# Where the second layer's later work stands in TensorE's order: fixed slots, or slots chosen by running estimates

## The chip, the cores and the metric

One core of a Trainium2 chip runs the whole computation in one launch. The metric is the device time of one execution in microseconds, from start to end, as the median of several runs. Five engines work side by side and meet through semaphores: TensorE (PE in the profile: matrix products and transposes), VectorE (DVE: elementwise work, reductions, reading results out of PSUM), ScalarE (ACT: functions such as Exp, and copies), GpSimd (POOL) and SyncE (SP, which issues the DMA transfers). Each engine takes the instructions of its own queue in order.

## The reference

The input x has 16 batches of 64 rows and 512 columns; a context has 16 batches of 1601 rows. Six residual stages follow one another:

```python
x = x + _L0_xattn_ref(_layernorm(x), ctx_1024, ...)
x = x + _L0_attn_ref(_layernorm(x), ...)
x = x + _L0_ffn_ref(_layernorm(x), ...)
x = x + _L1_xattn_ref(_layernorm(x), ctx_1024, ctx_1024, mask, ...)
x = x + _L1_attn_ref(_layernorm(x), ...)
x = x + _L1_ffn_ref(_layernorm(x), ...)
```

The first three (layer 0) are not touched here. The fourth is a cross attention with 16 heads of 32 columns over the 1601 context rows of the batch, with a mask, biases on all projections, and softmax. The fifth is a "differential" attention: each row forms a 32 by 32 table of products between its own 32 query groups and 32 key groups of 16 numbers, takes softmax along it, subtracts a learned multiple of one half from the other, multiplies with v, normalises, and goes through Wo; a LayerNorm and a feed-forward network (512 to 2048 to 512, with Relu) follow inside the same stage. The sixth is a feed-forward network with ternary weights (every weight rounded to -1, 0 or 1 times a scale), activations rounded to 8 bits with a scale for each row, and a convolution over three neighbouring rows and Silu between its two products:

```python
h = bit_linear(x, w1)
h = depthwise_conv1d(h.transpose(0, 2, 1), conv_w, conv_b).transpose(0, 2, 1)
return bit_linear(silu(h), w2)
```

## The kernel before

The layer-0 functions run first. Then `l1_layer` does the last three stages. Two batches make one tile t of 128 rows, so 16 batches b make 8 tiles. PE's instructions keep the order in which the program names them (`tc.manual_schedule(engines={PE})`). The queues of the other engines are put in order by a scheduler when the kernel is built, by its own estimate of when each instruction could start; after that every queue is fixed.

**The cross attention** is a run of 32 calls of `step(b, F, ...)`, two for each batch. F picks half of the heads: four score tiles p of 128 rows (two heads of 64 queries) by 1601 keys. A step does the following on PE, in this order:

- `turn` (transposes by `transpose_keys`, L182, copied out by ACT, L185) and `last_keys` (L888) turn the first two p tiles of the step before; blocks of `project_v` (products `wkv,ctxT` at L146, evacuated at L832) stand between; `attend` (L898) multiplies the weights with V into a bank of tag acc.
- `scores` runs four times, once for each piece of the keys (three of 384 and one of 449). It takes two PSUM banks of tag tp and two of tag mm and writes products of queries and keys into them (L873); DVE copies them into p where the mask allows it (`copy_predicated`, L880), which frees the banks. Tag tp has two banks, mm four, acc two. The transposes take tp banks too. V blocks and the turning of the other two p tiles stand between the four.
- a second `attend`, and when F is 0 the end of the batch before, `finish`: a small product that spreads the softmax sums (`fold`, L924), a multiplication on DVE that divides by them (oT, L934), on odd batches (so in the step of an even b) a bias on DVE (L940), then the output product py (L146 with `w,oT`), and `residual`.
- `weigh` for each p tile: the negative maximum of the rows on DVE (negm, L1318), then Exp on ACT (L1319). And 16 pieces of `project_k` (L803, evacuated by ACT at L811): keys for the next step.

**The later stages** of a finished tile are a generator, `later(t)`: LayerNorm, the q, k, v products (L146 with `w,hT`), 16 pairs of DVE instructions for q times k (`products`: a multiplication at L967 and a reduction at L968), the softmax along 32 (L1010 to L1033, with Exp on ACT at L1019), 8 pairs for att times v, the normalisation (ending at L1063), Wo, a LayerNorm, the feed-forward network with W1 and W2 (L1100), and the mark "fed". Then `last(t)`: LayerNorm and rounding, four parts of the ternary product (hs at L1207, a product with the middle tap on ACT into y at L1213, the two other taps on DVE at L1220 and L1224, Silu at L1230, a maximum at L1232), the largest value of each row over all parts (top, L1238, transposed at L1244), rounding (L1255, L1256) and the second ternary product (L1266) and the output. `queries(t)` makes the queries of the next tile, and `ternary_weights` rounds the ternary weights once, during the first batches.

Each `yield` ends a piece of such a generator. A `slot()` inside `step` runs one piece of `behind`, whatever the engines are doing; in the F=0 step of an even batch there are no slots before the batch's `finish` has run (`resting`), where `behind` is set to the `later` of the tile just finished. Where a piece depends on a slow step, additional bare `yield`s leave slots empty. At the end of each odd batch whatever is left of `behind` is run at once. In the last two batches one slot in three is left empty and `behind` stops at the mark "attended". The loops at the end of `l1_layer` take turns between the last tile (`final`, t=7) and the rest of the one before it.

The lines that the steps below speak of most:

```python
def slot():
    nonlocal places
    places += 1
    if resting == 0 and (b < B - 2 or places % 3):
        run(behind, 1)
```

Of the kernel before, what the change touches and what calls it, by code (L numbers as in the profile page):

```python
# [19 lines left out]
P = 128  # L20
# [13 lines left out]
EPS = 1e-5  # L34
# [403 lines left out]
def until(steps, mark):  # L438

    for x in steps:  # L440
        if x == mark:
            return
        yield
# [244 lines left out]
def l1_layer(g, d, out):  # L688
# [5 lines left out]
    with ExitStack() as es:  # L694
# [76 lines left out]

        def value_tile():
            nonlocal taken
            i = taken % (NV + 5)
            taken += 1
            if i < NV:
                return vpool.tile([P, 2, 256], F32, tag="v", name="v")
            return g.const.tile([P, 2, 256], F32, tag=f"x{i - NV}", name="v")
# [18 lines left out]
        def project_k(b, h):  # L797

            for n, (_, w) in enumerate(KC):
                for f in (h, h + 2):  # L800
                    ps = mm(g)
                    for c in range(NC):
# [4 lines left out]
                        if c == 1:  # L807
                            yield
                    tag = "kT" if n < 3 else "kT_last"
# [5 lines left out]
        def project_v(b, half):  # L815

            for k in range(0, len(KT), 2):
# [3 lines left out]
                for j, (k0, kw) in enumerate(blocks):  # L821
# [6 lines left out]
                    vs[b, half, k + j] = v[:kw, j, :]  # L828
                    if j + 1 < len(blocks):
                        yield  # L830
# [3 lines left out]

        def queries(t):

            u = apool.tile([P, D], F32, tag="u2", name="u")
            ln_apply(g, u, g.x[t], ln_stats(g, small, [g.x[t]]), 0)
            yield
            yield  # L840
            uT = apool.tile([P, NC, P], F32, tag="u2T", name="uT")
            nc.scalar.copy(uT, transpose4(g, u))
            yield
# [20 lines left out]
        def scores(b, F, n, ps_, mk):  # L864
# [5 lines left out]
            for r in range(4):  # L870
                for i in range(2):
# [6 lines left out]
                    )  # L878
            for p, bank in zip(ps_, banks):
                nc.vector.copy_predicated(p[:, k0 : k0 + w], mk[:, k0 : k0 + w], bank[:, :w])  # L880

        def last_keys(ps_, pTs):
# [4 lines left out]
            for j, p in enumerate(ps_):  # L887
                nc.tensor.transpose(pt[:kw, j, :], p[:, k0 : k0 + kw], g.ident)  # L888
                pTs[j].append(pT[:kw, j, :])
# [4 lines left out]


# [65 lines left out]
        def products(q, k, out, n):  # L961

            kv = k.rearrange("p (j d) -> p j d", d=16).unsqueeze(1).to_broadcast([P, CH, 32, 16])
            for i in range(n // CH):
# [5 lines left out]
                )  # L970
                yield

        def norm_T(src, gname, bname):

            z = apool.tile([P, D], F32, tag="z", name="z")
            ln_apply(g, z, src, ln_stats(g, small, [src]), 0)
            for _ in range(4):
                yield
            pt = transpose4(g, z)
            dst = apool.tile([P, NC, P], F32, tag="hT", name="hT", bufs=2)  # L980
# [7 lines left out]
        def later(t):  # L988

            u = apool.tile([P, D], F32, tag="u", name="u")  # L990
            ln_apply(g, u, g.x[t], ln_stats(g, small, [g.x[t]]), 0)
            yield
            hT = yield from norm_T(u, "ln1_g", "ln1_b")
            yield
            qkv = []
            for n, s in (("q", float(DA) ** -0.5), ("k", 1.0), ("v", 1.0)):
# [5 lines left out]
                yield  # L1002
# [9 lines left out]
            nc.vector.copy_predicated(raw, nan, zero.to_broadcast([P, 32 * 32]))  # L1012
            yield
# [4 lines left out]
            )  # L1018
            nc.scalar.activation(att, att, AF.Exp)  # L1019
            yield  # L1020
            yield
# [9 lines left out]
            yield  # L1031
            a2 = att[:, :HA, :HA]
            nc.vector.tensor_tensor(a2, a2, att[:, HA:, HA:], ALU.subtract)  # L1033
            yield
# [12 lines left out]
            nc.vector.tensor_tensor(o3, o3, inv.unsqueeze(2).to_broadcast([P, HA, 32]), ALU.mult)  # L1047
            sq = apool.tile([P, D], F32, tag="z", name="sq")
            nc.scalar.activation(sq, o, AF.Square)
            yield  # L1050
# [4 lines left out]
            nc.vector.tensor_scalar(r, r, 1e-6, None, ALU.max)  # L1055
            nc.scalar.activation(r, r, AF.Sqrt)
            yield
# [6 lines left out]
            for _ in range(4):  # L1064
                yield
            oT = apool.tile([P, NC, P], F32, tag="hT", name="oT", bufs=2)
            nc.scalar.copy(oT, transpose4(g, o))
            yield
# [4 lines left out]
            yield  # L1073
# [7 lines left out]
            for k in range(5):  # L1081
                if k < 4:
# [8 lines left out]
                    for f in range(4):  # L1091
                        nc.scalar.activation(
                            hids[k][:, f, :], ps[:, f, :], AF.Relu, bias=col(g, "b1", 4 * k + f)
                        )
                    yield
                if k > 0:
                    for f in range(4):
# [5 lines left out]
                        )  # L1103
                    yield
            nc.vector.tensor_tensor(g.x[t], po, g.x[t], ALU.add)
            yield "fed"
# [4 lines left out]
        def ternary_weights():  # L1111


            for n, name in enumerate(("w1T", "w2T")):
# [5 lines left out]
                for k in range(8):  # L1120
                    nc.vector.tensor_reduce(
                        part[:, k : k + 1], load(k), AX.XY, ALU.add, apply_absolute_value=True
                    )
                    yield
# [7 lines left out]
                for k in range(8):  # L1132
# [4 lines left out]
                    nc.vector.tensor_scalar(wb, w, MAGIC, None, ALU.subtract)  # L1137
                    dst = g.tern[4 * n + k // 2].rearrange("p (c n) -> p c n", c=NC)
# [38 lines left out]
        def last(t):  # L1177
            u = apool.tile([P, D], F32, tag="z", name="u")
            ln_apply(g, u, g.x[t], ln_stats(g, small, [g.x[t]]), 0)
# [10 lines left out]
            yield  # L1190
            yield
# [6 lines left out]
            yield  # L1198
            big = apool.tile([P, 4, P], F32, tag="u", name="big")
            sT = []  # L1200
            for k in range(4):
                w = load_ternary(k)
                ps = mm(g).rearrange("p (f x) -> p f x", f=4)
                for f in range(4):
# [364 lines left out]
```

## Time and profile before

| | us |
|---|---|
| three timed runs | 3416.5, 3417.17, 3418.84 |
| median | 3417.17 |
| the profiled execution | 3425.22 |
| its span in the trace | 3423.4 |
| layer 0, about | 0 to 830 |
| layer 1, about | 830 to 3423 |
| mean granted clock of PE | 0.961 |

The profiled execution is 8.05 us longer than the median. In the profile, a busy row gives an engine's time at work and its share of the span. Rows of a timeline give start, duration, engine, line, operation, written tile `<-` read tiles, shape and count (merged when equal instructions follow one another; the duration then is from the first start to the last end); in brackets is the idle time before the row and what ended it. Waits list an engine's line, what it waited for, total time, how often, and the longest. `PEclk`, or the granted clock, is the share of full clock speed that TensorE had.

### The profile page before, as it was taken

How to read it: one execution, taken by the hardware profiler on the slowest of the kernel's cores; microseconds unless marked ns; L12 is line 12 of the kernel's file. 1: busy time of each engine (PE TensorE's matmuls, PEld its weight loads, DVE VectorE, ACT ScalarE, POOL GpSimd, SP SyncE). 2: the span in 40 equal slices, each digit the busy share in tenths (PEclk: the TensorE clock that was granted, in tenths of full speed). 3: DMA queues.
4: the chain of work that ended last, by engine and by line, in shares of the span. 5: the costliest groups of instructions: out<-in, count | busy, mean ns of one | idle time of the engine just before them, and what ended most of it. 6: DMA issues, size and time to landing. Idle time of an engine off the chain costs nothing.

```text
span 3423.4 us, 51470 instructions
## 1 busy us (share of the span) xinstructions
PE 3125.6 (91%) x22000; PEld 2099.7 (61%) x22008; DVE 1624.4 (47%) x2614; ACT 1083.6 (32%) x1960; POOL 380.6 (11%) x339
## 2 busy tenths in 40 slices
PE   6999999898999999989998999999899999999816
PEld 3344445586677667667766766666677667667604
DVE  2121214113733754392467348454825773484285
ACT  1111011111333344333433343343334343433303
POOL 0000002243011010010101001100110010001000
PEclk9999999999899999999999999999999999999958
DMA  9988502596531214213320522242133205120405
GB/s 358 318 285 301 195 25 93 208 336 196 184 84 45 91 38 152 74 48 111 109 68 24 157 69 85 62 128 81 42 118 102 78 27 158 59 79 13 144 16 173
DMA packets 272293, 422.34 MB, mean 123 GB/s; under 512 B 22576, under 2 KB 168112, under 8 KB 272064
## 3 DMA queue, kind: packets, MB, share of 16 engines
q1 hardware_dynamic: 258928, 372.38, 33.4%
q0 software_dynamic: 13136, 46.67, 3.9%
q8 instruction: 173, 2.83, 0.3%
q14 instruction: 56, 0.46, 0.0%
HBM read 394.36 MB, written 24.64 MB: 122 GB/s over the span
## 4 chain that ended last, share of the span: by engine, by line
PE 64%; DVE 24%; DMA 4%; ACT 3%; issue 3%; POOL 1%; SPq 1%; POOLq 0%; ACTq 0%; DVEq 0%
PE ps_mm L146 26%; PE ps_mm L803 12%; DVE prod L967 7%; PE ps_acc L146 7%; DVE att L968 5%; PE ps_acc L1100 3%; PE ps_tp L182 3%; DVE negm L1318 3%; PE ps_mm L240 3%; DVE p L880 2%; PE ps_tp L873 2%; DVE o L968 2%; PE ps_acc L274 2%; PE ps_acc L898 2%; DMA ck<-in_ctx_dram 2%
## 5 line engine op out<-in xcount | busy, mean ns | idle before, releaser
L146 PE MATMUL ps_mm<-wkv,ctxT 128*128 128x256 f32 x2304 | 544.5, 384 | 1.0 <-DVE p L880 1.0
L803 PE MATMUL ps_mm<-ctxT,wkv 128*128 128x384 f32 x1536 | 520.2, 489 | 0.0
L146 PEld LDWEIGHTS ps_mm<-wkv,ctxT 128*128 128x128 f32 x2304 | 422.5, 191 | 91.6 <-issue 41.0
L803 PEld LDWEIGHTS ps_mm<-ctxT,wkv 128*128 128x128 f32 x1536 | 285.9, 191 | 181.7 <-issue 8.5
L1301 POOL MEMSET p<- 128x1601 f32 x128 | 184.1, 1441 | 1777.9 <-PE ps_tp L182 1105.8
L880 DVE COPY_PREDICATED p<-mk,ps_tp 128x384 f32<-128x384 uint8 (+1 forms) x256 | 143.9, 599 | 449.0 <-PE ps_mm L873 448.1
L832 ACT COPY v<-ps_mm 128x512 f32<-128x512 f32 (+1 forms) x224 | 123.0, 551 | 464.1 <-PE ps_mm L146 463.6
L185 ACT COPY pT<-ps_tp 128x512 f32<-128x512 f32 x384 | 206.7, 589 | 157.2 <-PE ps_tp L182 157.2
L146 PE MATMUL ps_mm<-wkv,ctxT_last 128*128 128x256 f32 (+1 forms) x1024 | 248.3, 386 | 1.0 <-ACT v L832 1.0
L182 PE MATMUL ps_tp<-ident,p 128*128 128x128 f32 x1640 | 217.8, 275 | 14.1 <-DVE p L880 9.1
L1318 DVE TENSOR_REDUCE negm<-p 128x1 f32<-128x1601 f32 x128 | 226.5, 1810 | 1.1
L1319 ACT ACTIVATE p<-p,negm 128x1601 f32<-128x1601 f32 x128 | 208.4, 1628 | 51.5 <-DVE negm L1318 49.5
L182 PEld LDWEIGHTS ps_tp<-ident,p 128*128 128x128 f32 x1640 | 191.2, 142 | 54.1 <-issue 18.5
L146 PEld LDWEIGHTS ps_mm<-wkv,ctxT_last 128*128 128x128 f32 (+1 forms) x1024 | 172.4, 178 | 72.2 <-issue 40.4
L803 PE MATMUL ps_mm<-ctxT_last,wkv 128*128 128x449 f32 x512 | 201.7, 539 | 0.0
L967 DVE TENSOR_TENSOR prod<-qkv 128x1024 f32<-128x1024 f32 x128 | 156.6, 1223 | 91.0 <-ACT qkv L1000 87.4
L811 ACT ACTIVATE kT<-ps_mm,cols 128x384 f32<-128x384 f32 x192 | 108.8, 574 | 192.5 <-PE ps_mm L803 192.5
L968 DVE TENSOR_REDUCE att<-prod 128x64 f32<-128x1024 f32 x128 | 155.9, 1218 | 3.9
L803 PEld LDWEIGHTS ps_mm<-ctxT_last,wkv 128*128 128x128 f32 x512 | 96.1, 190 | 87.1 <-issue 79.5
L898 PE MATMUL ps_acc<-pT,v 128*32 128x64 f32 (+1 forms) x6656 | 116.2, 228 | 32.0 <-ACT pT L185 31.0
L880 DVE COPY_PREDICATED p<-mk,ps_mm 128x384 f32<-128x384 uint8 (+1 forms) x256 | 138.8, 591 | 0.0
L898 PEld LDWEIGHTS ps_acc<-pT,v 128*32 128x32 f32 (+1 forms) x6656 | 103.5, 115 | 56.6 <-ACT pT L185 33.0
(302 smaller groups left out, 4003.3 us busy)
## 6 DMA issues: line engine op xcount, KB each, us to landing
ctxT<-in_ctx_T_dram SPq DMA_DIRECT2D x48, 1024.0 KB
ck<-in_ctx_dram SPq DMA_DIRECT2D x48, 1024.0 KB
ctxT<-in_ctx_T_dram SPq DMA_DIRECT2D x48, 768.0 KB
w<-in_W1T_dram SPq DMA_DIRECT2D x64, 512.0 KB
w<-in_W2T_dram SPq DMA_DIRECT2D x64, 512.0 KB
wt<-tern SPq DMA_DIRECT2D x64, 512.0 KB
ctxT_last<-in_ctx_T_dram SPq DMA_DIRECT2D x16, 898.0 KB
w<-in_x_Wq_dram SPq DMA_DIRECT2D x16, 512.0 KB
```

The source lines that it names most:

```text
L146: g.nc.tensor.matmul(out, lhsT=lhs(c), rhs=rhs(c), start=(c == 0), stop=(c == n - 1))
L182: g.nc.tensor.transpose(pt[:kw, j, :], p[:, k0 + j * P : k0 + j * P + kw], g.ident)
L185: (out_of or (lambda o, i: evac(g, o, i)))(pT[:kw, :blocks, :], pt[:kw, :blocks, :])
L803: nc.tensor.matmul(ps[:, :w], lhsT=wk[:, c, ts(f, P)], rhs=ctxs[b, n][:, c, :], start=(c == 0), stop=(c == NC - 1),)
L832: nc.scalar.copy(v[:kw, : len(blocks)], ps[:kw, : len(blocks)])
L880: nc.vector.copy_predicated(p[:, k0 : k0 + w], mk[:, k0 : k0 + w], bank[:, :w])
L898: nc.tensor.matmul(po[ts(r, HDX), ts(f, S)], lhsT=vs[b, f // 2, k][:, ts(4 * (r % 2) + 2 * (f % 2) + r // 2, HDX)], rhs=pTs[r // 2][k][:, ...
L967: nc.vector.tensor_tensor(pr, qv.unsqueeze(2).to_broadcast([P, CH, 32, 16]), kv, ALU.mult)
L968: nc.vector.tensor_reduce(out[:, ts(i, CH * 32)], pr.rearrange("p i j d -> p (i j) d"), AX.X, ALU.add)
L1301: nc.gpsimd.memset(p, -1e15)
L1318: nc.vector.tensor_reduce(negm, p, AX.X, ALU.max, negate=True)
L1319: nc.scalar.activation(p, p, AF.Exp, bias=negm, accum_out=sums[b][:, at : at + 1])
```

## The change

The fixed placing of the pieces is replaced by a running estimate. `g.now` is an estimate of PE's time and `g.dve` one of the time up to which DVE is loaded. Parts of the program add their own constants: `pe(us)` moves `g.now`; `dv(us)` moves `g.dve` from the later of both. A piece now ends with nothing, with a time before which the next may not be placed (`done()` after DVE's load, `soon()` after PE's time), or with a mark. A class `Work` holds a generator with its time; `may(backlog)` says whether its next piece may be placed: its time has come, and DVE's load is no more than `backlog` ahead of PE. A slot runs up to two pieces, of `asked` (the queries), else `old` (the end of the tile before), else `behind`.

Beside this:

- `norm` replaces the LayerNorm helpers in these stages and cuts them at ACT's Sqrt; pieces end ahead of ACT's steps in softmax and normalisation.
- The four ternary parts are put a step apart: seven steps, each with Silu of part step-2, the product of part step, the convolution of part step-1 and the maximum of part step-3. y alternates between the tags prod and att; the fourth sT goes to tag hT.
- `later(t-1)` is no longer run to its end at the end of an odd batch. At `finish` it is run on up to the mark "topped", then goes on as `old` while the next tile's `later` starts as `behind`; `old` is run to its end at the same place in the next batch.
- `weigh` of the four tiles moves from ahead of and between the first K pieces to the K pieces 2, 4, 6 and 8; the second part of `finish` moves to K piece 2; more slots stand between V blocks, each with its own backlog.
- `fetch` of a later tile's rows moves from the start of an even batch to the F=0 step of an odd one.
- The loops at the end are one loop: a piece of `final` has the first call until its mark "fed", then waits until the rest of the tile before is over.

The diff, cut to its core:

```diff
+class Work:
+    def __init__(self, g, steps):
+        self.g, self.steps, self.at, self.mark, self.over = g, iter(steps), 0.0, None, False
+        self.passed = set()
+    def may(self, backlog):
+        g = self.g
+        return not self.over and g.now >= self.at and g.dve - g.now <= backlog
+    def step(self):
+        x = next(self.steps, self)
+        self.over = x is self
+        self.passed.add(x if isinstance(x, str) else None)
+        self.mark = x if isinstance(x, str) else None
+        self.at = x if isinstance(x, float) else 0.0
+        if self.mark:
+            self.at = max(self.g.dve + 0.4, self.g.now + 1.6)
+    def rest(self, mark="over"):
+        while not self.over and mark not in self.passed:
+            self.g.now = max(self.g.now, self.at)
+            self.step()
...
+        def pe(us):
+            g.now += us
+        def dv(us):
+            g.dve = max(g.dve, g.now) + us
+        def done(us=0.1):
+            return max(g.dve, g.now) + us
+        def soon(us):
+            return g.now + us
...
@@ products
                 )
+                dv(2.5)
                 yield
...
@@ later: softmax
+            dv(2.5)
+            yield done()
             nc.scalar.activation(att, att, AF.Exp)
-            yield
-            yield
+            yield soon(2.2)
...
@@ last
-            for k in range(4):
-                w = load_ternary(k)
...
+            for step in range(7):
+                k = step - 2
+                if 0 <= k < 4:
...
+                    nc.scalar.activation(sT[k], y[k].rearrange("p f b s -> p f (b s)"), AF.Silu)
+                k = step
+                if k < 4:
+                    w = load_ternary(k)
...
+                k = step - 1
+                if 0 <= k < 4:
...
+                k = step - 3
+                if k >= 0:
+                    nc.vector.tensor_reduce(
+                        big[:, k, :], sT[k].rearrange("p f t -> p t f"), AX.X, ALU.max,
+                        apply_absolute_value=True,
                     )
+                    dv(0.8)
+                yield done(0.2 if 0 < step < 5 else 1.2)
             top = spool.tile([P, P], F32, tag="dg", name="top")
             nc.vector.tensor_reduce(top, big.rearrange("p f t -> p t f"), AX.X, ALU.max)
-            yield
-            yield
-            yield
-            yield
+            dv(0.8)
+            yield "topped"
...
@@ step
+            def slot(backlog=2.6):
+                nonlocal named
+                for _ in range(2):
+                    if asked.mark != "ready" and asked.may(backlog):
+                        asked.step()
+                    elif old.may(backlog):
+                        old.step()
+                    elif (
+                        not (behind.mark == "normed" and not old.over)
+                        and not (b >= B - 2 and behind.mark == "attended")
+                        and (b < B - 2 or g.now >= named + 2.5)
+                        and behind.may(backlog)
+                    ):
+                        named = g.now
+                        behind.step()
...
             for i in range(3):
                 value()
-                slot()
+                slot(1.6)
+                value()
+                slot(1.0)
                 if i == 2 and before is not None:
                     last_keys(p4[2:], tail)
-                value()
+                    value()
                 if before is not None:
                     turn(p4[2:], pTs, i)
-                value()
+                    slot(0.6)
+                if i < 2 or before is None:
+                    value()
                 scores(b, F, i + 1, ps_, mk)
+                slot(2.6)
...
-            weigh(0)
             slot()
-            run(keys, 2)
-            weigh(1)
-            if F == 0:
-                run(ending)
...
+            for i in range(16):
+                if i == 2 and F == 0:
+                    run(ending)
+                    pe(3.5)
+                    pos[b] = mm(g, tag="acc")
+                    if b % 2 == 0 and b > 0:
+                        behind.rest("topped")
+                        old, behind = behind, Work(g, later(b // 2 - 1))
+                    if b % 2 == 1:
+                        old.rest()
+                    if b % 2 == 1 and b + 1 < B:
+                        if 2 <= b // 2:
+                            fetch(b // 2 + 1)
+                        asked = Work(g, queries(b // 2 + 1))
+                if i >= 2 and F == 1 and asked.mark == "ready":
+                    asked.step()
+                    asked.step()
                 run(keys, 1)
+                if i in (2, 4, 6, 8):
+                    weigh(i // 2 - 1)
+                slot(3.2)
...
-            final = later(NT - 1)
-            feed = until(rest, "fed")
-            for _ in until(final, "attended"):
-                run(feed, 1)
-            run(feed)
-            for _ in until(final, "fed"):
-                run(rest, 3)
-            while next(final, final) is not final:
-                run(rest, 2)
-            run(rest)
+            final = Work(g, later(NT - 1))
+            passed, fed = set(), False
+            while not (final.over and behind.over):
+                if final.may(1.2) and (behind.over or "fed" not in passed):
+                    final.step()
+                    passed.add(final.mark)
+                elif behind.may(1.2) and ("attended" in passed or not fed):
+                    behind.step()
+                    fed = fed or behind.mark == "fed"
+                else:
+                    g.now += 0.1
```

## The prediction

> **What bounds the kernel now.** I read the page's busy shares first, then a table of stretches, then PE's waits, then the timelines around the longest of them. The shares:
>
> ```profile
> PE 3125.6 (91%) x22000; PEld 2099.7 (61%) x22008; DVE 1624.4 (47%) x2614; ACT 1083.6 (32%) x1960; POOL 380.6 (11%) x339
> ```
>
> TensorE (PE) is the bound, VectorE (DVE) has half its time free on average. The average hides stages. L1 repeats every two batches; from one set of p memsets to the next it takes 310.56 us. The table of stretches for one such period (its four steps, then the whole) and for the end of the kernel; columns are the stretch, its length, then busy time of PE, PE's weight loads, DVE, ACT, POOL, then granted clock, DMA share, GB/s:
>
> ```profile
> 1387.84:1466.35 78.51, 74.44 (x568) 54.45 (x567) 36.92 (x49) 27.75 (x50) 7.01 (x6) 0.98 0.20 63
> 1466.35:1528.48 62.13, 57.89 (x494) 40.15 (x493) 60.55 (x63) 24.15 (x40) 7.38 (x6) 1.00 0.19 57
> 1528.48:1627.20 98.72, 93.50 (x690) 67.37 (x689) 34.56 (x67) 34.26 (x69) 9.72 (x7) 0.97 0.31 97
> 1627.20:1698.08 70.88, 69.72 (x614) 49.80 (x614) 40.12 (x81) 35.48 (x64) 5.74 (x5) 1.00 0.39 120
> 1387.84:1698.40 310.56, 295.87 (x2362) 212.09 (x2362) 172.15 (x258) 121.96 (x220) 30.17 (x23) 0.98 0.28 86
> 3336.88:3378.90 42.02, 38.03 (x236) 28.27 (x238) 23.50 (x65) 17.79 (x44) 1.10 (x1) 0.90 0.71 231
> 3385.88:3423.40 37.52, 12.30 (x88) 8.11 (x89) 22.11 (x58) 11.48 (x24) 0.00 (x0) 0.68 0.21 76
> ```
>
> In the second step DVE is busy 60.55 of 62.13 us: there DVE, not PE, is full. PE's waits in that period:
>
> ```profile
> PE ps_acc L898 <- ACT pT L185: 5.2, 2, 4.9
> PE ps_tp L888 <- DVE p L880: 3.5, 1, 3.5
> PE ps_acc L146 <- DVE oT L940: 3.3, 1, 3.3
> ```
>
> With smaller ones they come to 14.5 us: all that better placing can save, besides clock. The third, on DVE's and on PE's timeline:
>
> ```profile
> 1416.88 1.82 DVE L1318 TENSOR_REDUCE negm<-p 128x1 f32<-128x1601 f32 x1
> 1418.62 0.67 DVE L880 COPY_PREDICATED p<-mk,ps_tp 128x449 f32<-128x449 uint8 x1
> 1419.17 1.19 DVE L880 COPY_PREDICATED p<-mk,ps_mm 128x449 f32<-128x449 uint8 x2
> 1420.26 5.25 DVE L1318 TENSOR_REDUCE negm<-p 128x1 f32<-128x1601 f32 x3
> 1425.43 0.41 DVE L934 TENSOR_TENSOR oT<-ps_acc,rb 128x256 f32<-128x256 f32 x1
> 1425.87 0.69 DVE L940 TENSOR_TENSOR oT<-oT,bv 128x512 f32<-128x512 f32 x1
> ```
> ```profile
> 1426.62 5.41 PE L146 MATMUL ps_acc<-w,oT 128*128 128x256 f32 x16 [3.31 <-DVE oT L940]
> ```
>
> The two instructions that PE needs stand behind four maxima (negm, 1.8 us each) in DVE's queue. And the 16 matmuls after the gap take 5.41 us, where the same form takes 3.67 elsewhere (1569.19 in the trace): about 1.75 us of clock go with it. So DVE's local queue, not its total, prices this change.
>
> **The change part by part.** Removed or added work: nearly none. PE's matmuls, products and softmax stay. I cost PE's work at 292 us a period in both kernels (310.56 less 14.5 of waits and 3.9 of clock loss behind them: 1.75 after the 3.31 us gap, 1.2 in attend and about .9 in the scores after the 4.90 us gap); the estimates themselves are Python and cost nothing on the chip. What changes is order, so I read the built queues of the changed kernel and added up rows of before.
>
> **1. The end of step b even, F=0** (six times, b=4 to 14). In the built order DVE has, after the last scores: four copies with the eight conv instructions of the last ternary part among them, negm, a reduction over sT, negm, top, negm, oT (L994), negm, oT plus bias (L1000). From rows: copies 2.5 (0.66, 0.67, 1.19); conv 2.2 (eight at the tail's pitch, 3390.82 to 3393.09); four negm 7.1; the reduction 1.03 and top 1.02 (3406.60, 3407.65); oT 1.1: 15.0 us, and 0.7 for a late hs, 15.7. PE's cover from the end of the scores to the product that needs oT is a V block 1.87, attend 1.6, the fold .94, one K tile 2.6: 7.0. So PE waits 8 to 8.7 us, against 3.3 now: +5.0, and +0.5 for the longer time at a slow clock: +5.5. Ends: +2 (part of the conv gets done before the copies) and +8 (the clock falls for all 16 matmuls and the K tiles behind). Six times: +33, ends +12 and +48. Waiting for py: the residual, and with it the next LN.
>
> The Trainium skill ("TensorE: Matmul & The Clock Gate", section "What's actually happening") says that an idle window of about 3.4 us halves the clock and that about 3.4 us of work restores it. Rows: after 3.31 us idle the matmuls lost 1.75 us, after 3.54 us the next two (0.43 us) show no loss, after 4.90 us attend takes 2.79 instead of 1.6. By the page a gap of 8.7 us costs 1.7 us as one of 4.9 does, so my +0.5 would be 0, six times, and the forecast 3 us lower.
>
> **2. The products of later(t)** (steps b even F=1 and b odd F=0). Now DVE runs from 1449.73 to 1542.58 without a pause, and PE waits .4, 3.5 and 4.9 us beside it: 8.8. After, the copies of the first scores of b odd stand behind 16 q.k pairs and four and a half of the eight att.v pairs. From k's evacuation DVE has: 20.5 pairs by 2.51 (rows of 1.23 and 1.22 with gaps), 51.4; four sets of copies 8.9; negm 7.2; softmax with its waits for ACT and POOL, mk .98 and wide 1.13, about 12.2: 79.7 us. PE's work over the same stretch, added from K tiles (2.6, last 3.02), V blocks (1.78), transposes (.87 per eight) and scores, is 69.3. The turn's transposes need the tp banks that these copies free, so PE waits at least 79.7 - 69.3, 10.4, and some 3 more follow: pT copies on ACT stand behind the Exp of att, which waits for DVE's subtraction, and 3.5 pairs are left. 13.8 against 8.8: +5.0. Ends: -5 (the gaps fall where PE has cover, as the before trace's negm after 1504.76 do) and +12 (the pT gap of 4.9 doubles and the clock falls twice). I count it six times of seven, since for b=14 and 15 pieces are at least 2.5 us apart by `named`: +30, ends -30 and +72.
>
> **3. The edits with one answer.** norm in pieces and ends ahead of ACT's steps: same instructions; ACT is busy 122 of 310 us, and a table load stays 1.28. y in tag att, sT[3] in hT: no added wait, since att is free once o is made. fetch moved: SP's queue holds it behind the previous output and Wv's load; a 256 KB row block at 123 GB/s takes 2 us and is read a step later, so K projection hides it; without that cover 2 us each, six times. `rest("topped")` raises g.now by up to 5.3 us of ternary PE work not yet done, so pieces behind it come early on DVE: this is in 1 and 2.
>
> **4. The end of the kernel.** Now FFN of t=7 and last(6) are mixed: 42.0 us from 3336.88, and last(7) takes the rest; 86.5 from the FFN's start to the end. In the built PE queue the whole FFN comes first, then all of last(6), then last(7). FFN alone: four W1 (3.6) and four W2 (3.5), 28.4, and 2.6 for the first W1 at the low clock (6.21 in the row): 31.0. last(6) from its transposes to its last product: 3385.88 to 3418.82, 32.9, less 2.7 for the parts a step apart (DVE's chain from hs to top is 19.8 us and holds 17.1 of work): 30.2. last(7) with the output: 37.5 less 2.7, 34.8, its LN under last(6). 96.0: +9.5. Ends +2 (last(7)'s DVE work moves into last(6)'s gaps) and +15: the sixteen loads of W1 and W2, 8.4 MB, would have to come at 270 GB/s to fit 31.0 us, and at the 231 of the row they take 36.3, 5 more.
>
> **Sum.** 33 + 30 + 9.5 = +72.5 on the profiled execution: its 3425.2 us (span 3423.4 and 1.8 around it) become 3497.7. That execution lies 8.05 us above the median of the three timed runs, so in their terms 3489.
>
> **The rivals.** *A: the placing does what it says* (other side). The waits of a period and the clock behind them, 14.5 and 3.9, go in 5.5 periods: -101, +9.5 at the end: 3425.2 - 101 + 9.5 - 8 = 3326. It decides if DVE has the copies and oT done before PE asks; for that the 79.7 must fall under 69.3, a place where four products fewer stand ahead. DVE's 172 busy us of 310 speak for it, its built queue against it. *B: parts 1 and 2 change nothing*, as gaps move from one place to another: only part 4, 3427. For it: both kernels have the same DVE work between k and the end of the products, and PE can only lose what DVE lacks. *C: gaps deepen*: at the upper ends of 1 and 2, +120, and 9.5: 3547. For it: scores at .92 instead of .55 after the 4.9 us gap.
>
> **How the numbers follow.** My forecast (3455 to 3530) has .60, A .12, B .16, C .12. A change of 0.2%, 6.8 us, is about what a measurement of this kernel can tell from none. A counts as faster, a quarter of B as faster and another quarter as same: faster .16, same .05, slower .79. The range must hold eight in ten: down to 3400 (leaves out A), up to 3545 (leaves out half of C).
>
> **What would show it.** Right: the period between sets of p memsets is about 321 us; a wait of the py product on oT (L1000) of 8 to 9 us six times, with DVE's sT reduction and top just before; waits of transposes on p and pT in F=1 of b even and F=0 of b odd that sum to 13 to 15; at the end tq of last(6) after the last W2 of t=7, and about 96 us from the FFN's start. Wrong: a period under 311 us with PE's waits under 10 would be A, and would mean that my sums took work on DVE as late that in fact ran ahead of PE; or py's product waiting less than 4 us, if the conv is done before the scores end.

## The result, and the profile after

The changed kernel takes 3474.39 us (median of four runs, 3473.69 to 3478.59) against 3418.01 of the kernel before (3416.5 to 3420.84): slower by 56.4 us, a ratio of 1.0167 with a 95% interval of 1.0149 to 1.0184. The forecast was 3489, with 3400 to 3545 as its range.

The busy shares of the page after hardly differ from those before: PE still fills nine tenths of the span, and no engine has more to do.

```profile
PE 3137.7 (90%) x22008; PEld 2100.5 (60%) x22008; DVE 1615.7 (47%) x2614; ACT 1063.6 (31%) x1946; POOL 377.7 (11%) x339
```

To see where the time went I cut both traces at the small `fold` product of each batch's `finish`. It occurs 16 times, always at the same point of the work.

| from fold to fold | before, us | after, us | difference |
|---|---|---|---|
| start to the 1st (layer 0 and the first batches) | 988.6 | 984.0 | -4.6 |
| 1st to 4th | 431.0 | 429.7 | -1.3 |
| 4th to 14th (five periods of two batches) | 1553.0 | 1585.3 | +32.4 |
| 14th to 15th (the last pair) | 145.6 | 159.7 | +14.1 |
| 15th to 16th | 97.5 | 97.4 | -0.1 |
| 16th to the end | 207.7 | 215.8 | +8.1 |
| sum: the spans | 3423.4 | 3471.9 | +48.5 |

The first row is layer 0, which is unchanged, and the first batch. It says nothing of the change: e2 and e5 below have the code of the kernel before there, and took 981.2 and 980.6 us. The profiled execution of before was 7.2 us above its median and that of after 0.7 below its own, which is why the spans differ by less than the medians. And some work crosses a cut. The second ternary product of a tile and what stands around it, 3.8 us on PE, comes half a period later in the changed kernel, so that the second row has it for tile 0 before and not after, and the row of the last pair for tile 5 after and not before. For the same work the second row is +2.5 and the last pair +10.3.

One period in the table of stretches, first of before, then the same period of after (columns as in the prediction):

```profile
2189.43:2500.03 310.60, 295.90 (x2367) 212.16 (x2361) 172.16 (x259) 121.94 (x220) 29.83 (x22) 0.98 0.28 86
```
```profile
2205.10:2522.00 316.90, 298.66 (x2369) 213.52 (x2361) 171.37 (x259) 119.21 (x218) 29.21 (x22) 0.98 0.27 84
```

DVE has no more work (171 us). PE is busy 2.8 us longer with the same matmuls, which is read here as slower clock, and idle 3.5 us longer. PE's waits in that period of after say where:

```profile
PE ps_acc L146 <- DVE oT L1000: 7.0, 1, 7.0
PE ps_tp L946 <- ACT pT L185: 5.6, 4, 4.6
PE ps_tp L946 <- DVE p L938: 1.8, 1, 1.8
PE ps_tp L182 <- DVE p L938: 1.3, 1, 1.3
PE ps_tp L182 <- ACT hT L1043: 1.2, 1, 1.2
```

The wait of the output product on oT has grown from 3.3 to 7.0 us; all others together come to 11.1 us, where they were 11.2. DVE's timeline at that place, from the end of the scores:

```profile
2363.92 0.34 DVE L1320 SCALAR_TENSOR_TENSOR y<-hs,cols,y 128x126 f32<-128x126 f32 x1
2364.17 0.60 DVE L1316 SCALAR_TENSOR_TENSOR y<-hs,cols,y 128x126 f32<-128x126 f32 x2
2364.69 0.60 DVE L1320 SCALAR_TENSOR_TENSOR y<-hs,cols,y 128x126 f32<-128x126 f32 x2
2365.21 1.81 DVE L1421 TENSOR_REDUCE negm<-p 128x1 f32<-128x1601 f32 x1
2366.95 1.03 DVE L1327 TENSOR_REDUCE big<-sT 128x128 f32<-128x512 f32 x1
2367.91 1.80 DVE L1421 TENSOR_REDUCE negm<-p 128x1 f32<-128x1601 f32 x1
2369.63 1.02 DVE L1334 TENSOR_REDUCE top<-big 128x128 f32<-128x512 f32 x1
2370.57 1.80 DVE L1421 TENSOR_REDUCE negm<-p 128x1 f32<-128x1601 f32 x1
2372.30 0.41 DVE L994 TENSOR_TENSOR oT<-ps_acc,rb 128x256 f32<-128x256 f32 x1
2372.63 1.80 DVE L1421 TENSOR_REDUCE negm<-p 128x1 f32<-128x1601 f32 x1
2374.36 0.67 DVE L1000 TENSOR_TENSOR oT<-oT,bv 128x512 f32<-128x512 f32 x1
```

and PE's product behind it:

```profile
2375.09 6.46 PE L146 MATMUL ps_acc<-w,oT 128*128 128x256 f32 x16 [7.01 <-DVE oT L1000]
```

DVE works without a gap, but in the wrong order for PE: the convolution of the last ternary part, its maximum, top and the negm stand ahead of the two instructions that PE waits for (three negm ahead of the first, the fourth between the two). The 16 matmuls then take 6.46 us instead of 5.41 before and 3.67 at full clock.

This is so in five of the six even batches, b=6 to 14, each with a wait of 7.0 us. In the first of the six, b=4, the ternary part and top were done before the scores ended, only the negm stood ahead of oT, and nothing was lost against the kernel before (3.31 and 5.41 us; `sc` was written in the same tenth of a microsecond as oT):

```profile
1420.31 5.41 PE L146 MATMUL ps_acc<-w,oT 128*128 128x256 f32 x16 [2.79 <-DVE sc L1223]
```

At the end of the kernel the table of stretches shows the serial order: the network of the last tile, then the ternary stage of tile 6, then that of tile 7.

```profile
3378.20:3409.20 31.00, 30.98 (x161) 23.24 (x162) 2.37 (x9) 5.57 (x19) 1.12 (x1) 0.90 0.72 233
3409.20:3439.40 30.20, 11.94 (x91) 6.98 (x90) 24.73 (x72) 11.28 (x25) 0.00 (x0) 0.66 0.40 137
3439.40:3471.90 32.50, 11.21 (x90) 6.65 (x88) 22.21 (x58) 9.90 (x23) 0.00 (x0) 0.74 0.30 103
```

DVE is nearly idle in the first (2.37 us of 31.00) and PE mostly idle in the other two.

### The profile page after: what moved, and what is told of

Read it like the earlier page. It is cut to its first block, busy times and chain, and to the rows that moved or that the text cites. A ratio compares the mean times of both kernels' runs of the same rounds, so it can differ in the third digit from the quotient of the medians.

```text
span 3471.9 us, 51444 instructions
## 1 busy us (share of the span) xinstructions
PE 3137.7 (90%) x22008; PEld 2100.5 (60%) x22008; DVE 1615.7 (47%) x2614; ACT 1063.6 (31%) x1946; POOL 377.7 (11%) x339
## 4 chain that ended last, share of the span: by engine, by line
PE 64%; DVE 25%; DMA 4%; ACT 4%; issue 2%; POOL 0%; SPq 0%; ACTq 0%; POOLq 0%; DVEq 0%
PE ps_mm L146 25%; PE ps_mm L836 14%; PE ps_acc L146 7%; DVE prod L1027 6%; DVE att L1028 4%; PE ps_acc L1173 3%; DVE p L938 3%; DVE negm L1421 3%; PE ps_mm L240 2%; PE ps_tp L182 2%; PE ps_tp L929 2%; PE ps_acc L274 2%; DVE o L1028 2%; PE ps_acc L958 2%; DMA ck<-in_ctx_dram 2%
## 5 line engine op out<-in xcount | busy, mean ns | idle before, releaser
L836 PE MATMUL ps_mm<-ctxT,wkv 128*128 128x384 f32 x1536 | 512.1, 488 | 0.6
L185 ACT COPY pT<-ps_tp 128x512 f32<-128x512 f32 x384 | 207.7, 592 | 125.5 <-PE ps_tp L182 125.0
L146 PEld LDWEIGHTS ps_mm<-hT,w 128*128 128x128 f32 x1024 | 122.1, 198 | 10.6 <-issue 6.5
L146 PE MATMUL ps_mm<-hT,w 128*128 128x128 f32 x1024 | 122.9, 281 | 1.2 <-ACT hT L1043 1.2
```

The costliest lines, as they stand in the source:

```text
L146: g.nc.tensor.matmul(out, lhsT=lhs(c), rhs=rhs(c), start=(c == 0), stop=(c == n - 1))
L185: (out_of or (lambda o, i: evac(g, o, i)))(pT[:kw, :blocks, :], pt[:kw, :blocks, :])
L836: nc.tensor.matmul(ps[:, :w], lhsT=wk[:, c, ts(f, P)], rhs=ctxs[b, n][:, c, :], start=(c == 0), stop=(c == NC - 1),)
```

## The experiments

The theory to test: the change costs its time at three places, the order of DVE's queue in front of oT, pieces placed earlier than the engines can take them, and the serial end. The main rival: PE's gaps are only moved about, so that taking one away brings another. All times below are medians; the kernel before took 3418 to 3420 us on the same chips.

**e1: oT ahead of the maxima, in the changed kernel.** An ordering edge on DVE's queue, F=0 steps only:

```diff
-            nc.vector.tensor_tensor(oT[:, :, ts(hb, S)], ...)
+            g.divided = nc.vector.tensor_tensor(oT[:, :, ts(hb, S)], ...)
...
+                behind_oT = F == 0 and before is not None
+                with tc.issue_after(g.divided.ins) if behind_oT else ExitStack():
                     nc.vector.tensor_reduce(negm, p, AX.X, ALU.max, negate=True)
```

> The changed kernel, with one edge added: in the F=0 steps, VectorE may not issue the four maxima (negm) before the division and bias that make oT. PE's order is untouched. Theory 1 (the end of the even batch costs what the prediction says, because the last ternary part, top and the maxima stand before oT in VectorE's queue): the wait of the py product falls from 7.0 us to under 1.5 us, six times, its 16 matmuls from 6.46 to about 3.7 us; with the seventh and the F=0 steps of odd batches unharmed that is 6 x (5.5 to 7 + 2.7), 50 to 58 us less than the 3474.4: 3416 to 3425. Theory 2 (the gap only moves: PE has nothing to gain since Exp and the next transposes come later by as much): within 10 us of 3474.

Measured: 3428.97 us (ratio to before 1.0023, 1.0011 to 1.0034), 45.4 us less than the changed kernel. PE's product on its timeline in e1:

```profile
2356.19 3.72 PE L146 MATMUL ps_acc<-w,oT 128*128 128x256 f32 x16 [1.20 <-DVE oT L1000]
```

The wait is 1.20 us instead of 7.01 and the matmuls run at full clock; a period takes 308.4 us instead of 316.9. So 45 us come back when DVE takes the work that it has anyway in another order; about half of them is a wait that the kernel before has too. In the four later periods and the last pair the edge takes 8.0 to 8.8 us each, and the other waits about kept their sizes: nothing moved. In the first of the five periods, where the wait was 2.8 us, it takes nothing (315.2 us for 315.3): PE waits 2.4 us for sc2i instead. With that period the 50 to 58 us of theory 1 were not reached.

**e2: the same edge in the kernel before.**

> The same edge in the kernel before. Theory 1: the seven waits of 3.3 us on oT go, and the 1.75 us by which the 16 matmuls behind each run slow: 7 x 5.05 = 35 us, 3383 against 3418. Theory 2 (the gap only moves): 3410 to 3425.

Measured: 3446.97 us (1.0076, 1.0059 to 1.0093), 27 us slower than without the edge: neither theory had that. The oT wait is gone. In its place PE waits for z, the input of a LayerNorm's transposes, twice a period:

```profile
PE ps_tp L126 <- DVE z L117: 6.8, 2, 4.1
PE ps_acc L898 <- ACT pT L185: 3.9, 2, 3.6
PE ps_tp L888 <- DVE p L880: 3.5, 1, 3.5
```

ACT's timeline shows why z is late:

```profile
2379.74 1.62 ACT L1321 ACTIVATE p<-p,negm 128x1601 f32<-128x1601 f32 x1
2381.26 0.19 ACT L1321 ACTIVATION_READ_ACCUMULATOR p<-p,negm 128x1 f32 x1
2381.47 1.28 ACT L98 ACT_TABLE_LOAD   x1
2382.76 0.20 ACT L98 ACTIVATE ln_rstd<-ln_rstd 128x1 f32<-128x1 f32 x1
```

The maxima come later, so the four Exp come later, and the Sqrt of the LayerNorm stands behind the last of them and a table load. That each of these engines takes its queue strictly in order is also what the Trainium skill says ("Perfetto Trace Analysis", section "Tensor Engine Instruction (MATMUL, LD_WEIGHTS)"). The rows of ACT above agree: the Sqrt's row starts behind the last Exp. In the changed kernel the same delay did no harm in e1, where PE has no wait on z; probably because there the transposes of z are placed by the estimates and not a fixed number of slots later, which no run tested by itself.

**e5: only two maxima behind oT, in the kernel before.**

```diff
-                behind_oT = F == 0 and before is not None
+                behind_oT = F == 0 and before is not None and r >= 2
```

> The kernel before, with only the third and fourth maximum of an F=0 step held back until oT is made, so that oT stands behind two maxima instead of four or none. Run e2, with none ahead, lost 27 us: its oT wait was gone, but PE then waited 4.1 and 2.75 us for z, whose place in PE's order is fixed. Theory 1 (z came late because all four Exp, and behind them on ScalarE the Sqrt of the LayerNorm, were put off by the edge): with two maxima ahead the Exp come almost as early as before, the oT wait falls from 3.3 to under 1, z waits under 1.5 us, and the time is 3385 to 3400. Theory 2 (z comes late whenever py comes early, since PE reaches z's fixed place as many us sooner as it no longer waits for oT): z waits 3 to 5 us again, and the time is 3415 to 3450.

Measured: 3416.22 us (0.9997, 0.9988 to 1.0007): no difference from before. z waits 1.4 us in all, as theory 1 had it, but oT still 2.1 us, because the copy rb that it needs stands on ACT behind two Exp. A period takes 310.6 us as before: the wait on oT is 1.2 us shorter, those on z are 1.0 longer, and the clock brings nothing, since the 16 matmuls behind the shorter gap still take 5.41 us in six of seven cases.

**e6: e2 with z two slots later.**

```diff
-            for _ in range(4):
+            for _ in range(6):
                 yield
             pt = transpose4(g, z)
```

> Run e2's kernel (all four maxima behind oT), with the transposes of a LayerNorm's z six slots behind it instead of four. Either theory of e2's loss says that z is then there when PE comes: waits on z under 1 us, and without them and the clock behind them 27 + 35 us less than e2's 3447, 3385 to 3400, if nothing else moves. If the loss of e2 was not z's fixed place, the waits on z or their loss reappear elsewhere and the time stays above 3420; pieces that come two slots later are also two slots closer to the end of the odd batch, where what is left is run at once.

Measured: 3417.48 us (0.9996, 0.9985 to 1.0007). It gives back e2's loss, which so hung on z's fixed place. But it stays at the level of before, short of the 3385 to 3400 expected: the waits on z fall to 1.9 us a period, and others come up (3.9 us for an oT of the later attention, 3.3 on p). In the kernel before, gaps do move, as the rival has it: with e5 and e6 a period takes 310.6 and 310.7 us, as without any edge. Why e6 comes to just the same was not settled.

**e3: the loops at the end of the kernel before, in the changed kernel.**

```diff
-            final = Work(g, later(NT - 1))
-            passed, fed = set(), False
-            while not (final.over and behind.over):
...
+            final = later(NT - 1)
+            rest = behind.steps
+            feed = until(rest, "fed")
+            for _ in until(final, "attended"):
+                run(feed, 1)
+            run(feed)
+            for _ in until(final, "fed"):
+                run(rest, 3)
+            while next(final, final) is not final:
+                run(rest, 2)
+            run(rest)
```

> The changed kernel with the loops at the end of the kernel before: the last tile's feed-forward network takes turns with the rest of tile 6 again. Theory 1 (the one loop costs the end 8.1 us, as the trace after shows from the last fold to the end, by putting tile 6's ternary stage wholly behind the network): 3466, with some 2.7 us more gained where the ternary parts a step apart now help: 3462 to 3468. Theory 2 (the end is set by VectorE and the transfers, and the order matters little): 3471 to 3478.

Measured: 3472.28 us (1.0158, 1.0141 to 1.0174), 2 us less; in the traces the end takes 212.4 instead of 215.8 us. Only 3.4 of the 8.1 us came back, and the time lies in theory 2's range. With three pieces of the ternary stage to one of the network, network and ternary stage mixed took about 50 us (42.0 before), with waits for W2 (1.8 us) and for q of the last tile (5.5). The old loop's fixed counts were made for other pieces, so this run did not tell what the serial order costs; e9 does.

**e4: ternary parts one after the other, in the changed kernel.** Short form of the edit:

```diff
-            for step in range(7):
+            for k in range(4):
...
+                yield done(1.2)
...
+                yield done(0.2)
...
+                yield soon(1.2)
```

> The changed kernel with the four ternary parts one after the other again, each with its own product, convolution, Silu and maximum, and the pieces' own estimated times. Theory 1: at the end of the kernel the two last ternary stages lose what the parts a step apart give, 2 x 2.7 us; in the middle more pieces with longer gaps push the end of a tile's ternary stage further into the next batch, and what is not done is forced at the end of the even batch: 3475 to 3500. Theory 2 (the parts a step apart are what puts the convolution and top in front of oT): the oT wait falls to about 3.3 us and the time to 3445 to 3455.

Measured: 3485.8 us (1.0199, 1.0182 to 1.0216), 11 us slower and in theory 1's range. The end takes 219.9 us, 4.1 more (5.4 expected). In the middle the oT wait falls to 2.4 us, as theory 2 had it, but PE now waits 4.7 us for top: the stage comes out later and its end is forced at the same place. The parts a step apart are a gain, and not what hurts.

**e8: PE's estimate no longer jumps, in the changed kernel.**

```diff
+                        now = g.now
                         behind.rest("topped")
+                        g.now = now
```

> The changed kernel, with only the jump of PE's estimated time taken back after the old tile is run on to top. Theory 1 (the jump brings pieces early and costs product waits): 12 to 30 us less than 3474, 3444 to 3462. Theory 2 (it does little): 3468 to 3480, with the oT wait still 7.0 us, since the pieces ahead of top are the same.

Measured: 3461.86 us (1.0132, 1.0115 to 1.0149), 12.5 us less. The 4.6 us wait on pT behind ACT's Exp of att is gone and a 4.6 us wait on p stands instead; p's 1.8 is 0.5 and the later 1.3 gone, 1.2 and 0.6 on p are new, and oT is at 7.0 as foreseen. A period takes 314.4 instead of 316.9 us. The time just lies in theory 1's range.

**e7: e1 with three estimates put right.** Beside e8's edit:

```diff
             nc.vector.tensor_scalar(mk, mk, 0.0, None, ALU.is_equal)
+            dv(1.0)
             return mk
...
+            dv(0.9)
             return wide
```

> Run e1's kernel (the changed one with oT ahead of the maxima, 3429), with three corrections of its estimates: the 5.3 us by which running the old tile on to top puts PE's estimated time ahead are taken back, and VectorE's load counts the mask's preparation (1.0) and the spreading of the sums (0.9). Theory 1 (the waits of 1.8, 4.6 and 1.2 us in the product stretch come from pieces placed too early, as the prediction's part 3 says): they fall to under 4 us together, with the clock behind them 4 to 6 us a period: 3400 to 3415. Theory 2 (the stretch holds 78 us of VectorE work against 72 of PE work in whatever order, so shifting its start by some us only moves the waits): 3422 to 3435.

Measured: 3411.4 us (0.9984, 0.9974 to 0.9993): 17.6 less than e1 and below the kernel before. The four larger waits of the product stretch still come to 7.4 us a period (8.3 in e1), so they did not fall as far as theory 1 said. A period takes 306.9 us for e1's 308.4, the first period 308.8 for 315.2, and the last pair, 151.4 us in e1, 147.1. How much each of the three corrections gives was not tested; e8 has the first alone, on another base.

**e10: half of the q times k products, in the changed kernel.** Every second pair is replaced by a small copy, the pieces keep their places; half of that table is then not computed.

```diff
             for i in range(n // CH):
+                if n == 32 and i % 2 == 1:
+                    nc.vector.tensor_copy(out[:, ts(i, CH * 32)], out[:, ts(i - 1, CH * 32)])
+                    dv(2.5)
+                    yield
+                    continue
```

> The changed kernel with the same pieces in the same places, but every second pair of the q times k products replaced by a copy of 64 columns (so half of that table is wrong): 8 x 2.3 us less VectorE work in the product stretch, nothing else. Theory 1 (PE's waits on p and pT in that stretch, 1.8, 4.6, 1.3 and 1.2 us, are there because VectorE has 78 us of work against PE's 72): they fall to under 2 us, and with the clock 7 to 9 us go in each of 6.5 periods: 3415 to 3430, with the wait on oT still 7.0. Theory 2 (those waits come from ScalarE's order, an Exp in front of the pT copies, whatever VectorE's load): the 4.6 us wait stays, and the time is above 3445.

Measured: 3432.66 us (1.0045, 1.0029 to 1.006), 42 us less. The end, where the products stand alone, gives 19.9 of it. Of the five periods the first gives 8.5 us and the others 3.0 to 4.5 each, less than 7 to 9: neither theory holds as it stood. The waits of 4.6 and 1.3 are gone, the 1.8 stays, and a new one of 2.5 us has come:

```profile
2438.91 0.66 PE L182 MATMUL ps_tp<-ident,p 128*128 128x128 f32 x4 [2.50 <-ACT pT L949]
```

With less to do DVE's queue was put in another order when built, with the softmax earlier, and ACT's Exp of att now stands in front of another copy that PE needs. So what PE waits for in this stretch depends on what stands ahead in a queue. How much the sum of DVE's work counts by itself this run can't tell, since the order changed with it.

**e9: e7 with the end mixed by estimates.** The two branches of the loop change places:

```diff
-                if final.may(1.2) and (behind.over or "fed" not in passed):
+                if behind.may(1.2) and ("attended" in passed or not fed):
...
-                elif behind.may(1.2) and ("attended" in passed or not fed):
+                elif final.may(1.2) and (behind.over or "fed" not in passed):
```

> Run e7's kernel (3411), and in the one loop at the end a piece of the tile before has the first call, so that tile 6's ternary parts stand between the last tile's W1 and W2 products. Theory 1 (the serial end costs what the prediction's part 4 says): from the start of the last feed-forward network to the end of tile 6's ternary stage 42 to 47 us instead of 61.3, less what the last tile's LayerNorm then has to wait (7 us, no longer under tile 6): 3398 to 3405. Theory 2 (as in run e3, mixing costs waits on weights and only some 3 us are gained): 3407 to 3411.

Measured: 3400.96 us (3393.89 to 3404.31; 0.9941, 0.9927 to 0.9954), faster than both kernels and in theory 1's range. Network and tile 6's ternary stage together, then the last ternary stage:

```profile
3317.07:3362.50 45.43, 40.51 (x244) 28.47 (x245) 27.12 (x75) 17.90 (x45) 1.09 (x1) 0.88 0.71 243
3362.50:3399.50 37.00, 13.95 (x96) 8.48 (x94) 23.48 (x64) 11.34 (x24) 0.00 (x0) 0.72 0.29 100
```

82.4 us instead of 93.7 in the changed kernel and 86.5 in the one before.

## Why the prediction was right, and where it was not

**Sign, place and size were right.** The 3474 lies inside the main case's own range (3455 to 3530). The places named are the ones that lose. The sum of +72.5 was some 16 us too high: part 1 by 10, part 2 by 11 over the five periods of the table, part 4 by 1; against that, 5 us in the last pair had been put at nothing.

**Part 1, the end of the even batch: right in kind, 23 us for 33.** Where it holds, PE waits 7.0 us, for 8 to 8.7 in the prediction, and the 16 matmuls behind take 5.92 to 6.74 us, on average 1.07 more than before, where it had 0.5: 3.7 + 1.07 = 4.8 for 5.5. But "six times, b=4 to 14" was five times. At b=4 the prediction's own condition for being wrong held, "py's product waiting less than 4 us, if the conv is done before the scores end". Five times 4.8, less the 0.5 by which that wait is shorter than before, are 23. In the period shown the stretch of DVE work is 14.2 us (2360.87 to 2375.09) for 15.0 to 15.7, since the late hs was already done, and PE's cover 7.2 for 7.0. e1 shows the cause: with the maxima behind oT the wait is 1.2 us and 45 us go, more than the 23, because the 3.3 us of the kernel before and the slow clock behind them go too.

**Part 2, the products: this step was mis-sized.** It had 13.8 us of waits a period against 8.8; in the period shown there are 8.9 (1.8, 4.6, 1.3 and 1.2). The part that was wrong is "PE's work over the same stretch ... is 69.3": from the end of k's product (2418.80) to the turn (2498.11) there are 79.3 us, of which PE is idle for 6.9, so its work was 72.4, with 1.6 of it slow clock behind the 4.6 us gap. DVE's chain up to the two copies that count was 78.3 us for 79.7. And where "some 3 more follow" there was a wait of 1.3. The difference of two sums near 75 us was 6 and not 10: errors of 4% and 2% on the two sums make nearly all of the +5.

The stretch wasn't free, though. When part 1 is taken out of the five periods of the table, 13.9 of the 32.4 us are left, where the prediction had 25: 5.3 us in the first, then 3.4, 1.5, 1.6 and 2.1. Most of this is no longer wait: PE is busy 2.7 to 3.7 us longer in a period, and at most 1.3 of that lies behind oT. That the rest is slower clock behind gaps that lie elsewhere is likely and was not tested by itself.

The prediction's "without a pause", for DVE from 1449.73 to 1542.58 in the kernel before, is not quite what the rows show either: they have pauses of 0.5 to 1.4 us. e10 adds that the difference of the two sums isn't the whole mechanism: with 16.6 us less on DVE (154.8 busy for 171.4) all of a period's waits together fell only from 18.1 to 15.6 us.

**The missing term: the last pair.** The product term was taken six times of seven, so that the last pair had only part 1's share. For the same work it lost 10.3 us, some 5 of them beyond part 1: waits of 18.7 us against 10.3, among them 7.4 on pT (3120.52 in the trace) where the later periods have 4.6. In e1 the pair takes 151.4 and in e7 147.1 us: 8.3 of the 159.7 go with the queue in front of oT (the kernel before has part of that wait too), and 4.3 with the estimates put right. The `named` spacing of 2.5 us did not keep the product stretch free there, as the prediction had assumed.

**Part 3, the jump of the estimate: right in kind.** "Pieces behind it come early on DVE": e8 takes only the jump away and gains 12.5 us. It was counted "in 1 and 2"; in part 1 it does nothing, since e8's waits on oT are still 7.0 us.

**Part 4, the end: right, 8.1 for 9.5.** 31.0 for the network (31.0 forecast), 30.2 for tile 6 (30.2), 32.5 for the last ternary stage (34.8 forecast: from its first transposes to those of top it took 18.2 us for 22.9 before, more than the 2.7 that the parts a step apart had been given). That the loads of 8.4 MB might stretch the first part to 36.3 us did not happen: 233 GB/s over 31.0 us are 7.2 MB, so some of the loads had landed ahead of it.

**The rivals.** A (all waits go, 3326) is out: the waits of a period rose from 14.5 to between 15.6 and 19.9 us. B (only the end, 3427) is out by the fold table: 43 us for the same work lie in the five periods and the last pair. C's deep clock loss is there at one place: 2.2 to 3.1 us behind each 7.0 us gap.

**The clock.** Behind the five gaps of 7.0 us the 16 matmuls took 5.92 to 6.74 us, on average 2.8 more than the 3.67 at full clock. By the rule that the prediction weighed from the Trainium skill ("TensorE: Matmul & The Clock Gate", "What's actually happening") the loss would be, as an estimate, 1.7 us whatever the gap. The measurement decides: behind the longer gaps of the changed kernel more was lost. The prediction's +0.5 was too small (1.07 on average), and the rule's 0 further off. But the same gap cost very different amounts, as the last section shows, so neither figure is a rule.

Over all, the runs lead from the changed kernel to a better one in three steps: 45.4 us (oT first), 17.6 (honest estimates), 10.4 (mixed end). Together 73 us, of which 56 are the change's own loss. (Medians of different chips; by the ratios to the kernel before on the same chip the steps are 49, 13 and 15 us.) So corrected, the changed kernel is some 17 us faster than the one before, and the scheduler's order in DVE's queue, three numbers and the last loop hid this. How much of the 17 is the placing by estimates, and how much what came with it (the ternary parts a step apart, which e4 prices at 11 us), was not told apart. Each correction was tried on top of the ones before, so the split among them holds in this order only.

## What to carry to other kernels

When one engine's order is written by hand and another's is left to a scheduler, read the built queue in front of each instruction that the first engine waits for; here two short instructions behind 7 us of maxima that nobody needed yet cost 45 us of 3474, some of it in the kernel before as well. A planner that places work by estimates must not move its clock for time that the engine doesn't spend (12.5 us here), and should count everything that the engine does. Where slots are fixed, taking one gap away can cost more than the gap, as e2 shows, because the work behind it, here z, was spaced for it.

## What the runs showed of the hardware

PE's clock after a gap did not follow the gap's length alone. In e4 the 16 matmuls of the output product stand behind a gap of 2.4 us five times, in the batches b=4 to 12. Twice they took 5.41 us and three times 3.72; behind gaps of the same 2.39 us there is one of each:

```profile
2052.20 5.41 PE L146 MATMUL ps_acc<-w,oT 128*128 128x256 f32 x16 [2.39 <-DVE oT L1000]
```
```profile
2371.22 3.72 PE L146 MATMUL ps_acc<-w,oT 128*128 128x256 f32 x16 [2.39 <-DVE oT L1000]
```

In e5 a gap of 2.06 or 2.07 us was followed by 5.41 us six times out of six. In the kernel before, 3.31 us always cost 1.75 us, while 3.54 us cost the next matmuls nothing (0.43 us for two, as after 1.81 us). Longer gaps cost more on average, with a wide spread: in the changed kernel 4.6 us cost about 1.6 us (0.69 and 3.25 us for what takes 0.43 and 1.89), and 7.0 us cost 2.2 to 3.1; in e8, with the same 7.0 us, the 16 matmuls took 5.33 to 6.76 us, a loss of 1.7 to 3.1:

```profile
2682.68 5.33 PE L146 MATMUL ps_acc<-w,oT 128*128 128x256 f32 x16 [7.01 <-DVE oT L1000]
```

Two gaps of 2.75 and 4.1 us in e2, in place of one of 3.3, left PE busy 2.3 to 5.1 us longer in a period (298.2 to 301.0 us in five periods, 295.9 before): splitting a gap did not make it cheaper there. What decides whether a gap costs anything stays open.
